# A graph network on one core: queries made with the table's rows and kept beside the residual rows, norms with shared roots

## The chip, the cores and the metric

The kernel runs on 1 core of a Trainium2 chip as one launch. The metric is the device time in microseconds (us). A core has five engines with queues of their own: TensorE (PE; its weight loads are listed as PEld), VectorE (DVE), ScalarE (ACT), GpSimd (POOL, which here issues the gathers and scatters by index) and SyncE (SP, which here issues most transfers). Matmuls write to PSUM, everything else works from SBUF, and transfers (DMA) move data to and from the chip's memory (HBM).

## The reference

There are 6250 nodes with 64 features, 200000 edges sorted by their target, and 64 features per edge.

```python
x = layernorm(x + L0(x, edge_weight, src, dst))      # attention over edges, max and mean of features, a gate
# L1, on that x:
edge_attr = mlp(ln(edge_embed))
for l in range(3):
    h = ln(x)
    q = h[dst] @ Wq[l];  kn, vn = h[src] @ Wkn[l], h[src] @ Wvn[l]
    ke, ve = edge_attr @ Wke[l], edge_attr @ Wve[l]      # all in 8 heads of 8
    alpha = (q * (kn + ke)).sum(-1) / scale
    alpha = softmax of alpha over the edges of one target
    agg = sum over a target's edges of (vn + ve) * alpha
    gate = sigmoid(agg @ Wih[l] + h @ Whh[l])
    x = x + (agg + gate * (h @ Wself[l] - agg)) @ Wout[l]
    x = x + mlp(ln(x))
return layernorm(x + ln(x_after_3_layers) * ng + nb)      # this x: the input of L1
```

(The biases are left out here; the kernel has them.)

## The kernel before

Nodes are sorted by their number of edges and cut into 49 blocks of 128 (the last, LB, has fewer nodes; the spare places of its 128 rows take edges of block 0's fullest nodes). A node of a block sits on a partition, and its edges are slots along the free axis, so a block has a rectangle of 128 x SL[b] edge slots (24 slots that are summed from a table in SBUF, plus 12 to 32 whose rows are gathered or handled with them).

Stage A (0 to about 4780 us) computes L0, the edge features (edge_attr, written to memory in the blocks' slots as `ea_d`), one-hot matrices `oh_d`, and for each block the first layer's inputs by `prepare`. Its order is a written-out schedule over ORDER.

Then come the three layers of L1, in a loop over the blocks in LORDER (L53) as a software pipeline written out by hand: an iteration works on five blocks at once, b (newest) to b4 (oldest), and the order of the calls is the order on every queue.

- `begin` (L1243) loads, for the block of the next iteration, `hv` (the normed features, transposed, with a row of ones) and `xb` (residual rows, from `x1_d` in layer 0 and `x2_d` after it), in layer 2 also `xv` from `x1_d`. The table `ftb` in SBUF holds the blocks' rows of k and v for a layer; `refill` (L1253) fills it from `tab`.
- For block b, TensorE first makes the query `q` (L1489) from `hv` into a PSUM tile `b_qe`, then `sums` makes k and v of the edges in groups of up to 8 slots: edge features by weights (L1310, f32), table rows by one-hot matrices (L1329, bf16, three parts to a number), gathered rows (L1317). ScalarE copies k and v out (L1333, L1336). `scores` (L1340, L1341) multiplies k by q and reduces on VectorE.
- `gather` (L1233) lets GpSimd fetch up to 12 rows of 128 (one `indirect_dma_start` for each) from the table `tab`, into one of 4 buffers; it is called after a part that used such a buffer. One call's gathers are a burst.
- b1: `soft` (L1345 on: maximum, exponent into the same PSUM tile `b_qe`), `values` (L1353 on: weighted sum).
- b2: `turned`, `gate`, `gated` (four VectorE instructions after a tanh, L1397 on), `update` (L1406, L1407).
- b3: `updated` adds the update to the residual rows (L1410) and norms them (`norm`, L531, ten VectorE instructions on 64 columns or on one); `turned2` (L559), `hidden` (L1421, L1423), `close` (L1428 on) adds the MLP's result.
- b4: `prepare` (L573) makes the next layer's inputs: a norm, a transposition (L589) into `fht` with its store, the product with the k and v weights (L601, 128 columns) that ScalarE copies twice (L602, L603), three bf16 parts of it (L608, L611, L614), and the store of the row into `tab`. The norm and the first step are issued from `close`, while the block is still b3. In layer 2 `close` norms twice instead, with the affine of ng, nb and the residual between them (L1437 on), and `put` (L1455) scatters the rows to the output, by index on GpSimd.

The six steps of L1497 to L1501 are spread over the groups of block b, so that TensorE has sums to do between them. Stores of a block are kept in a list `stores` and issued on SP by `flush` at the end of an iteration. Inverse roots are computed on VectorE by two Newton steps (`rsqrt`, L515), whose products are one instruction each for one column (L523) and two for more (L525, L526).

## Time and profile before

| | us |
|---|---|
| median of 3 runs | 10610.52 (10577.22 to 10615.33) |
| profiled execution | 10601.41 |
| its span | 10599.5 |
| layer 0, about | 4830 to 6733 |
| layer 1, about | 6733 to 8632 |
| layer 2, about | 8632 to 10600 |
| PE busy (PEld beside it) | 6784.7 (4613.5) |
| DVE busy | 5774.5 |
| ACT busy | 3190.8 |
| POOL busy | 3983.4 |

The mean granted clock of TensorE was 0.753 of full speed over the whole, and 0.77 to 0.79 in the layers. The profile's lines name a group of equal instructions by source line, engine, operation, output and input; "<-" after a wait names what ended it. "issue" is time in which an engine waited for nothing that the profile shows, "remote" an event that it can't tie to a work of this core. The 40 slices of the span stand as tenths of busy time:

```profile
PE   2544645555555555576677777677777766677776
DVE  5544545544555555553556555455665545666666
POOL 5244333333333333313434444343444434434442
```

Stage A ends in the eighteenth or nineteenth slice; the layers are the rest. TensorE is the busiest engine there.

### The profile page before, as it was taken

The page shows a single profiled execution, that of the slowest core. Times are in us where ns is not written, and L with a number is a line of the kernel's source. Part 1 is how long each engine was busy: PE and PEld are TensorE (multiplying, and loading weights), DVE is VectorE, ACT ScalarE, POOL GpSimd, SP SyncE. Part 2 cuts the span into 40 slices and gives each one's busy share as a digit, 9 for nine tenths or more (in the row PEclk, how much of TensorE's full clock was granted, in tenths as well). Part 3 has the DMA queues.
Part 4 walks back from the last instruction along what each step waited for, and adds up shares of the span by engine and source line. Part 5 has one row for each costly group of instructions (what it writes and reads, how often), then busy time and mean ns, then how long its engine had stood idle before and what let it go on. Part 6 is the DMA issues. An engine that isn't in the chain of part 4 may idle for free.

```text
span 10599.5 us, 163737 instructions
## 1 busy us (share of the span) xinstructions
PE 6784.7 (64%) x62377; PEld 4613.5 (44%) x62377; DVE 5774.5 (54%) x14777; ACT 3190.8 (30%) x6591; POOL 3983.4 (38%) x4201
## 2 busy tenths in 40 slices
PE   2544645555555555576677777677777766677776
PEld 1212222222222222234566666455666655565565
DVE  5544545544555555553556555455665545666666
ACT  1322323322333333342233333223333322222222
POOL 5244333333333333313434444343444434434442
PEclk6676767777777777787787888777778777787877
DMA  4333333333333333334444444444444444444443
GB/s 102 94 89 92 95 89 96 92 90 95 92 91 93 92 91 92 91 87 138 122 128 133 136 136 134 125 123 129 133 134 136 135 130 118 119 126 125 129 127 86
DMA packets 1118549, 1183.96 MB, mean 112 GB/s; under 512 B 669364, under 2 KB 821433, under 8 KB 1110719
## 3 DMA queue, kind: packets, MB, share of 16 engines
q1 hardware_dynamic: 652271, 705.16, 23.3%
q0 software_dynamic: 174624, 393.35, 14.5%
q10 hardware_dynamic: 290864, 74.87, 3.4%
q8 instruction: 502, 8.22, 0.3%
q14 instruction: 288, 2.36, 0.1%
HBM read 936.40 MB, written 236.44 MB: 111 GB/s over the span
## 4 chain that ended last, share of the span: by engine, by line
PE 53%; another core or an unknown queue 19%; issue 17%; ACT 5%; DVE 3%; DMA 1%; POOL 0%; SPq 0%; ACTq 0%; POOLq 0%; DVEq 0%
PE b_pk L1329 18%; PE b_pk L1310 12%; PE f_ph L982 6%; PE b_pk L1317 4%; PE f_tr L945 4%; PE f_pe L964 3%; ACT f_hid L986 2%; ACT s_bc L827 1%; ACT ea L968 1%; PE p_pm L824 1%; ACT f_sq L747 1%; PE p_pm L1421 1%; ACT f_xt L949 1%; PE p_pm L1430 1%
## 5 line engine op out<-in xcount | busy, mean ns | idle before, releaser
L1239 POOL DMA_INDIRECT g<-tab,fidx x2328 | 2245.7, 965 | 3530.2 <-PE b_pk L1317 1720.3
L728 POOL DMA_INDIRECT g<-ft_d,si x1596 | 1522.5, 954 | 2843.0 <-PE e_pt L1045 2370.4
L1329 PE MATMUL b_pk<-ftb,ohl 128*128 128x128 bf16 x21168 | 1889.7, 255 | 881.0 <-issue 830.5
L1329 PEld LDWEIGHTS <-ohl 128*128 128x128 bf16 x21168 | 1592.1, 116 | 1190.5 <-issue 1118.4
L1310 PE MATMUL b_pk<-fwkv,eal 64*128 64x128 f32 x12990 | 1390.8, 316 | 491.0 <-issue 460.2
L1340 DVE TENSOR_TENSOR b_k<-b_k,b_qe 128x768 f32<-128x768 f32 (+6 forms) x711 | 542.0, 762 | 1690.4 <-ACT b_k L1333 1143.9
L964 PE MATMUL f_pe<-f_hid,fw 128*64 128x448 f32 (+4 forms) x2464 | 770.9, 645 | 1080.1 <-ACT ea L968 563.4
L1333 ACT COPY b_k<-b_pk 128x384 f32<-128x384 f32 (+2 forms) x1011 | 475.5, 470 | 3072.4 <-remote 1455.5
L1310 PEld LDWEIGHTS b_pk<-fwkv,eal 64*128 64x128 f32 x12990 | 1064.4, 208 | 719.2 <-issue 634.5
L982 PE MATMUL f_ph<-f_xt,fw 64*128 64x448 f32 (+4 forms) x2464 | 826.1, 678 | 457.8 <-ACT f_xt L949 382.3
L949 ACT ACTIVATE f_xt<-f_tr,feg 128x352 f32<-128x352 f32 (+10 forms) x392 | 253.8, 648 | 2220.2 <-remote 1913.5
L1333 ACT COPY b_v<-b_pk 128x384 f32<-128x384 f32 (+2 forms) x1011 | 872.8, 863 | 0.0
L986 ACT ACTIVATE f_hid<-f_ph,fb 128x448 f32<-128x448 f32 (+4 forms) x1232 | 725.5, 635 | 448.7 <-PE f_ph L982 281.0
L964 PEld LDWEIGHTS f_pe<-f_hid,fw 128*64 128x64 f32 x2464 | 155.1, 149 | 1570.2 <-issue 849.6
L945 PE MATMUL f_tr<-f_mv,f_xs 128*64 128x44 f32 (+10 forms) x12544 | 557.7, 249 | 396.0 <-issue 349.7
L932 DVE TENSOR_TENSOR f_mv<-s_tt,e_fac 128x704 f32<-128x704 f32 (+10 forms) x392 | 349.7, 892 | 778.9 <-remote 663.2
L945 PEld LDWEIGHTS f_tr<-f_mv,f_xs 128*64 128x64 f32 x12544 | 506.3, 160 | 506.1 <-issue 430.4
L982 PEld LDWEIGHTS f_ph<-f_xt,fw 64*128 64x128 f32 x2464 | 261.7, 212 | 822.0 <-ACT f_xt L949 501.2
L1341 DVE TENSOR_REDUCE b_al<-b_k 128x96 f32<-128x768 f32 (+6 forms) x711 | 542.9, 764 | 24.5
L1360 DVE TENSOR_REDUCE b_ag<-b_v 128x64 f32<-128x2816 f32 (+17 forms) x147 | 455.5, 3099 | 5.1
L1359 DVE TENSOR_TENSOR b_v<-b_v,b_qe 128x2816 f32<-128x2816 f32 (+17 forms) x147 | 454.1, 3089 | 0.0
L1317 PE MATMUL b_pk<-g,oh 128*128 128x384 bf16 (+3 forms) x2358 | 446.7, 326 | 0.0
(403 smaller groups left out, 7784.8 us busy)
## 6 DMA issues: line engine op xcount, KB each, us to landing
ohl<-oh_d SPq DMA_DIRECT2D x882, 256.0 KB
eal<-ea_d SPq DMA_DIRECT2D x324, 384.0 KB
oh_d<-s_oh SPq DMA_DIRECT2D x294, 256.0 KB
g<-tab,fidx POOLq DMA_INDIRECT x2328
eal<-ea_d SPq DMA_DIRECT2D x93, 320.0 KB
ea_d<-ea ACTq DMA_DIRECT2D x114, 256.0 KB
eal<-ea_d SPq DMA_DIRECT2D x114, 256.0 KB
ea_d<-ea ACTq DMA_DIRECT2D x130, 224.0 KB
```

What stands on the lines that cost most here:

```text
L728: nc.gpsimd.indirect_dma_start(out=g[:, k - k0, :], out_offset=None, in_=t0_d[:], in_offset=bass.IndirectOffsetOnAxis(ap=got[b]["si"][:, k ...
L945: nc.tensor.matmul(pv[r * D : (r + 1) * D, j], xss[(4 * ORDER.index(b) + 4 * j0 // D) % 4][:, (j0 + j) % (D // 4), :], mv[:, j, :, r::2], ...
L964: nc.tensor.matmul(pe[h * D : (h + 1) * D, :w], w2[:, s, :], hid[s][:, h, :w], start=(s == 0), stop=(s == 1))
L982: nc.tensor.matmul(ph[h][:, :w], w1[r, s * P : (s + 1) * P], xf[r, e0 * D : e1 * D], start=True, stop=True)
L986: nc.scalar.activation(hid[s][:, h, :w], ph[h][:, :w], AF.Relu, bias=b1[:, s : s + 1])
L1239: nc.gpsimd.indirect_dma_start(out=g[:, t - t0, :], out_offset=None, in_=tabs[l % 2][:], in_offset=bass.IndirectOffsetOnAxis(ap=idx[:, f : ...
L1310: nc.tensor.matmul(pk[:, j % 2, j // 2, :], ea[r, e, :], w["wkv"][r], start=(j < 2), stop=False)
L1317: nc.tensor.matmul(pk[:, h, :c, :], ohs[l, b, NW][:, 0, :], rows_[:, slice(t, t + 2 * c - 1, 2), i, :], start=False, stop=(i == 2))
L1329: nc.tensor.matmul(pk[:, h, j, :], o, rows[:, i, :], start=False, stop=(j == c - 1 and q == len(us) - 1 and i == 2))
L1333: nc.scalar.copy(to.rearrange("p (j h) d -> p h j d", h=2), pk[:, :, : n // 2, d0 : d0 + D])
L1340: nc.vector.tensor_tensor(k, k, m["q"].unsqueeze(1).to_broadcast([P, k1 - k0, D]), ALU.mult)
L1341: nc.vector.tensor_reduce(m["al"][:, :, k0:k1].rearrange("p h k -> p k h"), k.rearrange("p k (h d) -> p k h d", h=H), AX.X, ALU.add)
```

## The change

- **The order of blocks** (LORDER): four of the blocks with the fewest edges lead, where two did.
- **The query**: `prepare` makes q, k and v in one product of 192 columns; its q columns are stored beside the residual rows (`x1_d`, `x2_d`, now 128 columns wide, by one DMA more on SP, in `stores`), and `begin` loads both in one transfer. The query's matmul of the layers (L1489) goes; `scores` reads q from SBUF. PSUM's `b_qe` keeps the exponents only. `b_x` and `xv` have a buffer more.
- **Norms**: the norm after the update (b3) and the next layer's norm (b4), in layer 2 also the two closing norms (of b4 and b5), are made together at the iteration's start, after `soft` of b1 and before its `values`, with one inverse root of two or three columns. `close` only adds (and stores); the second closing norm comes one iteration later, and the last block's alone. The affine of layer 2 takes three VectorE instructions, the norm's own last one included, instead of four.
- **gated** takes three VectorE instructions; only the first reads PSUM.
- **Steps**: `turned` of b2 is issued before b4's step, and `gate` and `gated` of b2 before `turned2` of b3.

```diff
-LORDER = (LB, LB - 1) + tuple(b for i in range(24) for b in ((1, 0, *range(2, 24))[i], LB - 2 - i)) [:-1]
+LORDER = (LB, LB - 1, LB - 2, LB - 3) + tuple(b for i in range(23) for b in ((1, 0, *range(2, 23))[i], LB - 4 - i))[:-1]
...
-x1_d = [dram.tile([P, D], F32, name=f"x1_{b}_d") for b in range(NB)]
-x2_d = [dram.tile([P, D], F32, name=f"x2_{b}_d") for b in range(NB)]
+x1_d = [dram.tile([P, 2 * D], F32, name=f"x1_{b}_d") for b in range(NB)]
+x2_d = [dram.tile([P, 2 * D], F32, name=f"x2_{b}_d") for b in range(NB)]
...
+def norms(wk, items):
+    k, mvs = len(items), []
+    for v, _ in items:
+        s6 = wk.tile([P, 6], F32, name="n_s6", bufs=4)
+        mvs.append(s6)
+        nc.vector.bn_stats(s6, v)
+    mv = wk.tile([P, k, 2], F32, name=f"n_mv{k}")
+    for j, s6 in enumerate(mvs):
+        nc.vector.bn_aggr(mv[:, j], s6)
+    vv = wk.tile([P, 2, k], F32, name=f"n_vv{k}")
+    for i, f in enumerate((KC, KC * K1 * K1)):
+        nc.vector.tensor_scalar(vv[:, i], mv[:, :, 1], f, f * EPS, ALU.mult, ALU.add)
+    r = rsqrt(wk, vv, k, f"n{k}")
+    for j, (_, put) in enumerate(items):
+        put(mv[:, j, 0:1], r[:, j : j + 1])
...
-def prepare(wk, mps, w, b, xb, i, hn=None):
+def prepare(wk, mps, w, b, xb, i, xd, hn=None):
...
-    kf = wk.tile([P, W1], F32, name="p_kf")
+    kf = wk.tile([P, 3 * D], F32, name="p_kf")
...
     def rows():
-        pm = mps.tile([P, W1], F32, name="p_pm")
-        nc.tensor.matmul(pm, ht, w["wc"][:, D : 3 * D], start=True, stop=True)
+        pm = mps.tile([P, 3 * D], F32, name="p_pm")
+        nc.tensor.matmul(pm, ht, w["wc"][:, : 3 * D], start=True, stop=True)
-        nc.scalar.copy(part[:, 0], kf)
+        nc.scalar.copy(part[:, 0], kf[:, D:])
+        stores.append(lambda: nc.sync.dma_start(xd[b][:n, D:], kf[:n, :D]))
+        if b == 0:
+            stores.append(lambda: nc.sync.dma_start(xd[LB][LN:P, D:], kf[:SPARE, :D]))
-    nc.vector.tensor_tensor(rest, kf, part[:, 0], ALU.subtract)
+    nc.vector.tensor_tensor(rest, kf[:, D:], part[:, 0], ALU.subtract)
...
-        stores.append(lambda: nc.sync.dma_start(x1_d[b][:], xb))
-        yield from prepare(wk, mps, nxt, b, xb, 0, hn)
+        stores.append(lambda: nc.sync.dma_start(x1_d[b][:, :D], xb))
+        yield from prepare(wk, mps, nxt, b, xb, 0, x1_d, hn)
...
     def begin(l, b):
-        xb = wk.tile([P, D], F32, name="b_x", bufs=6)
-        nc.sync.dma_start(xb, (x1_d if l == 0 else x2_d)[b][:])
+        xq = wk.tile([P, 2 * D], F32, name="b_x", bufs=7)
+        nc.sync.dma_start(xq, (x1_d if l == 0 else x2_d)[b][:])
-            xv = wk.tile([P, D], F32, name="xv", bufs=6)
-            nc.sync.dma_start(xv, x1_d[b][:])
-        ms[b] = dict(hv=hv, xb=xb, xv=xv)
+            xv = wk.tile([P, D], F32, name="xv", bufs=7)
+            nc.sync.dma_start(xv, x1_d[b][:, :D])
+        ms[b] = dict(hv=hv, xb=xq[:, :D], q=xq[:, D:], xv=xv)
...
         def gated(b, m):
-            nc.vector.scalar_tensor_tensor(gt[:, 1], at, 0.5, pg[:, 0], op0=ALU.mult, op1=ALU.add)
-            nc.vector.scalar_tensor_tensor(gt[:, 2], at, -0.5, pg[:, 0], op0=ALU.mult, op1=ALU.add)
-            nc.vector.tensor_mul(gt[:, 2], gt[:, 2], gt[:, 0])
-            nc.vector.tensor_add(gt[:, 1], gt[:, 1], gt[:, 2])
+            nc.vector.scalar_tensor_tensor(gt[:, 1], gt[:, 0], 1.0, pg[:, 0], op0=ALU.add, op1=ALU.mult)
+            nc.vector.scalar_tensor_tensor(gt[:, 2], gt[:, 0], -1.0, at, op0=ALU.add, op1=ALU.mult)
+            nc.vector.scalar_tensor_tensor(gt[:, 1], gt[:, 2], -0.5, gt[:, 1], op0=ALU.mult, op1=ALU.add)
-        def updated(b, m):
-            nc.vector.tensor_add(m["xb"], m["xb"], m["po"][:, :D])
-            m["h2"] = wk.tile([P, D], F32, name="b_h2")
-            norm(wk, m["h2"], m["xb"])
+        def plain(to, v):
+            return v, lambda mean, r: nc.vector.tensor_scalar(to, v, mean, r, ALU.subtract, ALU.mult)
+        def normed(b3, b4, b5):
+            items = []
+            if b3 is not None:
+                m = ms[b3]
+                nc.vector.tensor_add(m["xb"], m["xb"], m["po"][:, :D])
+                m["h2"] = wk.tile([P, D], F32, name="b_h2")
+                items.append(plain(m["h2"], m["xb"]))
+            if b4 is not None:
+                m4 = ms[b4]
+                xb = m4["xb"]
+                if l < 2:
+                    hn = wk.tile([P, D], F32, name="p_hn")
+                    items.append(plain(hn, xb))
+                else:
+                    y = m4["y"] = wk.tile([P, 2, D], F32, name="b_y", bufs=3)
+                    nc.vector.tensor_add(m4["xv"], m4["xv"], gb[:, 1, :])
+                    def close_(mean, r):
+                        nc.vector.scalar_tensor_tensor(y[:, 1], xb, mean, gb[:, 0, :], op0=ALU.subtract, op1=ALU.mult)
+                        nc.vector.scalar_tensor_tensor(y[:, 0], y[:, 1], r, m4["xv"], op0=ALU.mult, op1=ALU.add)
+                    items.append((xb, close_))
+            if b5 is not None:
+                y5 = ms[b5]["y"]
+                items.append(plain(y5[:, 1], y5[:, 0]))
+                last.append((b5, P if b5 < LB else LN, y5))
+            if items:
+                norms(wk, items)
+            if b4 is not None and l < 2:
+                m4["next"] = prepare(wk, mps, nxt, b4, xb, (l + 1) % 2, x2_d, hn)
+                m4["then"] = next(m4["next"])
+            if l == 2 and b4 == LORDER[-1]:
+                norms(wk, [plain(y[:, 1], y[:, 0])])
+                last.append((b4, P if b4 < LB else LN, y))
...
-                nc.sync.dma_start(x2_d[b][:], xb)
-                m["next"] = prepare(wk, mps, nxt, b, xb, (l + 1) % 2)
-                m["then"] = next(m["next"])
-                return
-            y = wk.tile([P, 2, D], F32, name="b_y", bufs=3)
-            norm(wk, y[:, 0], xb)
-            nc.vector.tensor_mul(y[:, 0], y[:, 0], gb[:, 0, :])
-            nc.vector.tensor_add(y[:, 0], y[:, 0], gb[:, 1, :])
-            nc.vector.tensor_add(y[:, 0], y[:, 0], m["xv"])
-            norm(wk, y[:, 1], y[:, 0])
-            n = P if b < LB else LN
-            last.append((b, n, y))
+                nc.sync.dma_start(x2_d[b][:, :D], xb)
...
-            b, b1, b2, b3, b4 = [LORDER[i - k] if 0 <= i - k < NB else None for k in range(5)]
+            b, b1, b2, b3, b4, b5 = [LORDER[i - k] if 0 <= i - k < NB else None for k in range(6)]
...
-            do(b3, updated)
+            normed(b3, b4, b5 if l == 2 else None)
...
-                m["q"], m["ex"] = qe[:, :D], qe[:, D : D + c * H].rearrange("p (h k) -> p h k", h=H)
-                nc.tensor.matmul(m["q"], m["hv"], w["wc"][:, :D], start=True, stop=True)
+                m["ex"] = qe[:, : c * H].rearrange("p (h k) -> p h k", h=H)
...
-            steps = [lambda: (do(b4, then), do(b2, turned)),
-                     lambda: (do(b3, turned2), do(b2, gate, gated)), lambda: do(b4, more, then),
+            steps = [lambda: (do(b2, turned), do(b4, then)),
+                     lambda: (do(b2, gate, gated), do(b3, turned2)), lambda: do(b4, more, then),
```

Only changed lines are shown, with four leading spaces less.

## The prediction

> **What bounds the kernel now.** I read the windows of the three layers first, then TensorE's waits, then the timeline around one burst of gathers, then the groups of the instructions the change touches. Stage A (to about 4780 us) changes only by a wider product and a few stores. Columns: stretch and its length, then busy time (and count) of PE, PEld, DVE, ACT, POOL, then granted clock, DMA share, GB/s.
>
> ```profile
> 4830.00:6733.00 1903.00, 1424.23 (x14105) 1134.40 (x14102) 1079.59 (x2312) 572.69 (x1337) 720.36 (x746) 0.79 0.48 134
> 6733.00:8632.00 1899.00, 1416.78 (x14049) 1133.22 (x14048) 1079.90 (x2310) 564.99 (x1321) 750.27 (x778) 0.78 0.47 131
> 8632.00:10600.00 1968.00, 1388.08 (x13862) 1106.43 (x13860) 1199.96 (x2835) 526.16 (x1125) 791.43 (x821) 0.77 0.43 119
> ```
>
> TensorE is busy 75% of a layer (1424 of 1903), VectorE 57%, DMA under half. What TensorE waits for in 4900 to 10600 (us in total, times, longest):
>
> ```profile
> PE b_pk L1329 <- issue: 851.0, 1149, 2.5
> PE b_pk L1310 <- issue: 459.7, 614, 2.5
> PE p_pm L559 <- DVE b_h L540: 38.9, 9, 10.1
> PE b_qe L1489 <- issue: 23.4, 26, 1.8
> PE p_pm L589 <- DVE p_hn L540: 19.7, 8, 2.8
> PE b_pk L1329 <- DMA ohl<-oh_d: 17.5, 2, 9.8
> ```
>
> VectorE stops TensorE only some 60 us in all, in a few waits; 1,311 us (851 + 460) are "issue", waits for nothing recorded. The timeline says when they come. First GpSimd, then TensorE, in the same ten microseconds:
>
> ```profile
> 6505.38 0.95 POOL L1239 DMA_INDIRECT g<-tab,fidx  x1 [15.65 <-PE b_pk L1317]
> ...
> 6514.18 0.95 POOL L1239 DMA_INDIRECT g<-tab,fidx  x1 [0.30 <-issue]
> 6517.27 0.95 POOL L1239 DMA_INDIRECT g<-tab,fidx  x1 [2.13 <-remote]
> ```
>
> ```profile
> 6510.51 0.43 PE L1489 MATMUL b_qe<-fwc,hv 65*128 65x64 f32 x2
> 6510.88 0.64 PE L1310 MATMUL b_pk<-fwkv,eal 64*128 64x128 f32 x4
> 6512.57 0.47 PE L1310 MATMUL b_pk<-fwkv,eal 64*128 64x128 f32 x2 [1.05 <-issue]
> 6514.03 0.27 PE L1310 MATMUL b_pk<-fwkv,eal 64*128 64x128 f32 x1 [0.99 <-issue]
> 6515.44 0.37 PE L1310 MATMUL b_pk<-fwkv,eal 64*128 64x128 f32 x1 [1.15 <-issue]
> ```
>
> About 5 us after a burst of gathers begins, TensorE starts to issue one or two matmuls per gap of a microsecond, and goes on normally a little after the burst. Over all bursts its gaps above 0.5 us add up to 2.8 us for a burst of 5 gathers, 5.8 for 8, 8.4 for 10, 12.4 for 12, 19.5 for 20: about 1.2 us per gather less 3.7. I call this the stutter. So the layers are TensorE's own instructions plus a stutter that the number and grouping of gathers sets. The change leaves the number alone (776 per layer). What can pay is TensorE instructions outside the stutter, and the ends of layers, where there is no next block to fill TensorE:
>
> ```profile
> 6701.89 0.42 PE L589 MATMUL p_pm<-fident,p_hn 128*64 128x128 f32 x1 [2.12 <-DVE p_hn L540]
> 6704.78 0.39 PE L559 MATMUL p_pm<-fident,b_h 128*64 128x128 f32 x1 [2.14 <-DVE b_h L540]
> ```
>
> **The change part by part.** The groups (count | busy us, mean ns | idle before):
>
> ```profile
> L1489 PE MATMUL b_qe<-fwc,hv 65*128 65x64 f32 x290 | 64.4, 297 | 23.5 <-issue 23.4
> L601 PE MATMUL p_pm<-fwc,fht 65*128 65x128 f32 x196 | 44.4, 310 | 1.1 <-ACT fht L590 1.1
> L1407 PE MATMUL p_pm<-fwout,b_gt 64*128 64x64 f32 x294 | 66.0, 300 | 16.3 <-issue 14.1 <-DVE b_gt L1402 1.3 <-PE p_pm L1406 0.9
> L1340 DVE TENSOR_TENSOR b_k<-b_k,b_qe 128x768 f32<-128x768 f32 (+8 forms) x707 | 539.0, 762 | 1651.2 <-ACT b_k L1333 1104.7 <-issue 298.0 <-ACT b_k L1336 245.2
> L1347 DVE TENSOR_TENSOR b_al<-b_al,fam 128x352 f32<-128x352 f32 (+17 forms) x146 | 76.6, 525 | 1.9
> L523 DVE TENSOR_SCALAR n_t<-n_y,n_vv 128x1 f32<-128x1 f32 x686 | 187.2, 273 | 25.2
> ```
>
> *The query product goes (L1489).* 147 blocks times 2 matmul records, 294. From the start of one to the start of TensorE's next instruction, 238 took at most 0.35 us, 42.4 us together (0.178 each); the other 56 lie in the stutter, 65.2 us together. The first 42.4 are on the path and go. In the stutter the gap belongs to the gathers: another matmul takes the place, and what is saved is that one's ordinary step, 56 x 0.178 = 10 us at most; I take half. Term: -48. Bounds: 0, if it all goes into longer stutter, and -108 (42.4 + 65.2), if the gaps go with their instruction.
>
> *192 columns instead of 128 in prepare's product (L601)*, 147 blocks (49 in stage A, 98 in two layers), 2 records each. In the layers TensorE's step from such a matmul to the next is 202 ns at 128 columns; at 64 (L1407) 201, at 384 (L964, edge features) 207. The width doesn't show in the step. Term 0; bounds 0 and +20, the latter from the mean duration of L964, 645 ns at 448 columns, against 310 here: 335 ns over 320 columns, 67 per 64, x 294. ScalarE copies half as much again; it is busy 30% of a layer, so nothing.
>
> *The q rows' store and the wider load.* One more DMA on SP's queue per block in prepare, 0.32 to 0.36 us to issue; it stands ahead of the table rows' store in the same list, and that waits for VectorE's last part anyway. Behind it are the next block's loads, issued an iteration ahead of their use. Layer 2 has no such stores and stutters no less. In stage A 49 x 0.45 us = +22 is the upper bound; term 0, since TensorE and VectorE there don't wait for SP. The load of residual rows doubles (64 KB for 32, 147 times, 4.8 MB, at a DMA share of 0.48): hidden by being asked for an iteration early; else the residual add would wait for it.
>
> *Scores read q from SBUF (L1340).* Both inputs of the multiply are then in SBUF. The row that is nearest is L1347, two SBUF inputs: of 86 gathers that began within such an instruction 70 took longer, 19.4 us together. Of 102 that began within L1340 (q in PSUM), with 39.5 us of it still to run, none was lengthened. At L1347's rate (19.4 of 31.0 us remaining) that is 25 us more of GpSimd in bursts, and the stutter lasts as long as the burst. Bounds 0 and +40; I take half of the 25, +12, since a stutter already begun may only shift. The multiply itself: L1355 from PSUM takes 519 ns and L1349, the same reduction from SBUF, 522; so no change.
>
> [...]
>
> *Shared norms and gated.* A norm is ten VectorE instructions, 2.45 us from its first to the next instruction (L523 among them at 273 ns). Two with shared roots come to some 3.6 us instead of 4.9, the three of layer 2 to 5 instead of 8.1 (with its affine in fewer instructions); gated loses one of four, 0.3 us. So VectorE does 1.6 us less per block in layers 0 and 1 and 3.5 less in layer 2. In the steady state nothing waits for it: TensorE's waits on L540 above are nine and eight, all in the drains. There VectorE is nearly always busy (6660 to 6705, and 10500 to 10585), and the last blocks' chains, norm to transpose to product, are serial. Worked through, a drain wins about 4 us at each of two layer ends; the last one wins 7, after paying for one norm more that comes alone there. Term: -15; bounds -30 and +10 (the norm now waits for two adds, so the earlier of the pair is late).
>
> *The moved steps.* Norms come after soft(b1) and ahead of values(b1), as the first norm did. The closing norms move to the next iteration's start, ahead of the transposition L589 that was already its first step. Gate before turned2, and turned before then: TensorE swaps neighbours; gated's L1399 waits for the tanh 418 us in all today with nothing behind it that TensorE needs within 1.5 us. Term 0, in those bounds.
>
> *The order of blocks.* Four light blocks lead each layer instead of two. The start burst is 33 gathers instead of 34, the 9.8 us wait for one-hot rows comes from weights' loads that stay, and the last three blocks swap places. Term 0, bounds +-15.
>
> **Sum**, on the profiled execution: 10601.4 - 48 - 15 + 12 = 10550. It was 9 us under the median of the runs shown, 10610.5; to that 10550 is -0.57%.
>
> **The rivals.**
>
> *Nothing reaches the end.* TensorE's 48 us are taken up by stutter: the burst is triggered by TensorE's progress, so with fewer instructions between bursts more of what remains falls into them. For it: five sixths of TensorE's lost time is stutter (1,311 us of 1,541 not busy). Against: the stutter's length goes with the count of gathers, whatever instructions fall in it. Then only drains and lengthened gathers are left, -15 + 12: 10598.
>
> *A larger gain.* All 108 us of the query product go, and the drains give 15: 10478. For it: 26 of the gaps end at L1489 itself (23.4 us of issue). Against: the same gaps end at L1310 and L1329 when these are next.
>
> *Bursts merge (slower).* In 95 of some 106 pairs a block's second burst follows the first by 2.1 us, as at 6517.27: its release at about 6510.2 comes 4.8 us after the first began, while TensorE's signals go unseen from about 4.3 us on. If TensorE is half a microsecond earlier there, the bursts join to one of 16, whose stutter is 1.2 x 16 - 3.7 = 15.5 against 2 x 5.8 = 11.6, and the pause between is lost: some 4.3 us a pair. It costs as much as this change gives from 12 pairs on, and makes the kernel slower by over 0.5% (10663) from 26 pairs; a third of them (35) gives 10700. For it: the margin is small, and the steps between were reordered. Against: the query product stands after that release, not ahead of it.
>
> **How the numbers follow.** About 0.5% is what a measurement of this kernel can tell from no change: 10557 to 10663. Forecast 0.48 (10520 to 10580, of which two thirds are under 10557); nothing reaches the end 0.20; larger gain 0.13; merged bursts 0.19. Faster: 0.31 + 0.13 = 0.44. Same: 0.17 + 0.20 = 0.37. Slower: 0.19. The range goes from the larger gain, 10470, to 10650: that leaves out most of the merged bursts and the edge of the larger gain.
>
> **What would show it.** No L1489; prepare's matmul with 192 columns and a step of about 0.2 us. Layers of 1885, 1882 and 1945 us in the windows. TensorE's issue waits on L1310 and L1329 at 1,290 to 1,340 us; at 1,360 or more the first rival or the merging holds, and pauses of 2.1 us between bursts that are gone tell which. Mean duration of gathers in the layers up by 10 ns (25 us over 2,328) if the multiply holds them up. DVE busy down by some 150 to 200 us with little to show for it. The prediction is wrong if TensorE shows new waits on the norms (L559 or L589 in the middle of layers), or if stage A is longer by more than 10 us.

## The result

| | before | changed |
|---|---|---|
| median of 12 runs each (us) | 10603.47 | 10632.12 |
| lowest to highest | 10577.22 to 10615.33 | 10612.6 to 10642.61 |
| profiled execution's span | 10599.5 | 10629.3 |
| stage A, to the first matmul of layer 0's sums | 4849.0 | 4870.2 |

The ratio is 1.003, with a 95% interval of 1.0023 to 1.0038: slower by 0.3%, where 0.57% less had been forecast. That is within the half per cent that the prediction calls no change, and on the other side of it.

A second pair of profiles, from chip 13 (median of the changed kernel 10626.9, ratio 1.0023, 1.0014 to 1.0033), lets me average. Between the two kernels the span grows by 32.2 us: stage A 19.6 more; from the first to the last matmul of the sums, layer 0 9.9, layer 1 19.7 and layer 2 5.7 more; the two stretches between layers 9.0 less together; the end, from the start of the last sum, 13.7 less (66.0 to 52.3).

The layers' windows of the changed kernel, with the columns of the prediction's first fence:

```profile
4851.00:6756.00 1905.00, 1398.88 (x14005) 1091.61 (x14004) 991.53 (x2073) 583.30 (x1337) 728.99 (x746) 0.78 0.48 135
6756.00:8673.00 1917.00, 1397.00 (x13938) 1095.10 (x13938) 991.18 (x2071) 574.68 (x1321) 761.84 (x778) 0.78 0.47 131
8673.00:10629.00 1956.00, 1361.22 (x13776) 1061.95 (x13775) 1009.21 (x2214) 529.15 (x1125) 804.04 (x822) 0.77 0.43 121
```

TensorE is busy for 72 us less in the three layers (4157 for 4229) and VectorE for 368 us less (2992 for 3359), and the layers are no shorter: 5778 for 5770 us. TensorE's waits of the changed kernel in the layers say where the time went (L1349 is the old L1329, L1330 the old L1310, L606 and L576 the old L589 and L559):

```profile
PE b_pk L1349 <- issue: 1256.8, 1616, 2.6
PE b_pk L1330 <- issue: 213.8, 318, 6.3
PE p_pm L606 <- DVE p_hn L1429: 29.1, 8, 5.6
PE b_pk L1349 <- DMA ftb<-tab: 13.3, 2, 7.0
PE p_pm L576 <- DVE b_h L1429: 6.2, 3, 3.2
```

"issue" on the two sums is 1,471 us where it was 1,311; the waits on norms (L606, L576) lie at the ends of the layers, but for one of 1.0 us. The 160 us are more than the 72 us saved.

The same in steps, each from the start of a matmul to the start of the next, from layer 0's first sum to layer 2's last, averaged over two profiles of each kernel: steps of at most 0.35 us fell from 3533 to 3461 us together, longer ones rose from 2150 to 2248 us. So TensorE's ordinary work gave 72 us, and the longer steps, most of them stutter (1953 of 2152 us in the first profile of before), took 98.

GpSimd's gathers, of the kernel before and then of the changed one (count | busy us, mean ns | idle before):

```profile
L1239 POOL DMA_INDIRECT g<-tab,fidx x2289 | 2208.6, 965 | 3329.4 <-PE b_pk L1317 1720.3 <-issue 620.9 <-PE p_pm L1406 455.8
```

```profile
L1259 POOL DMA_INDIRECT g<-tab,fidx x2295 | 2246.1, 979 | 3396.3 <-PE b_pk L1337 1779.8 <-issue 627.3 <-PE p_pm L1425 451.7
```

They are 14 ns longer each. And pairs of bursts join. Here is one, first the start of the second burst in the kernel before, with a pause of 2.40 us, then the same pair in the changed kernel's timeline, ten gathers from 8024.45 and the second burst after 0.31 us:

```profile
7938.26 0.95 POOL L1239 DMA_INDIRECT g<-tab,fidx  x1 [2.40 <-remote]
```

```profile
8024.45 0.95 POOL L1259 DMA_INDIRECT g<-tab,fidx  x1 [16.42 <-PE b_pk L1337]
...
8036.03 0.95 POOL L1259 DMA_INDIRECT g<-tab,fidx  x1 [0.30 <-issue]
8037.29 1.06 POOL L1259 DMA_INDIRECT g<-tab,fidx  x1 [0.31 <-issue]
```

Of 108 pairs beyond the heavy blocks 0, 1 and 2, one was joined before, 14 and 12 in the two profiles of the changed kernel. To price them I took, for each of 93 pairs that stand alone in both kernels, the window from the first gather to 8 us after the last, less the usual steps of the matmuls that began in it: what TensorE lost there. The second profile of before differs from its first by 1.5 us over all 93 together, so this measure repeats well. The newly joined pairs lost 48 and 39 us more (3.3 each); the 78 to 80 pairs that did not change state lost 53 and 57 more (0.7 each).

### The profile page after: what moved, and what is told of

It reads as the page before. It is cut to its first block, busy times and chain, and to the rows that moved or that the text cites. A ratio compares the mean times of both kernels' runs of the same rounds, so it can differ in the third digit from the quotient of the medians.

```text
span 10629.3 us, 162212 instructions
## 1 busy us (share of the span) xinstructions
PE 6733.2 (63%) x62083; PEld 4496.9 (42%) x62083; DVE 5409.1 (51%) x13678; ACT 3220.5 (30%) x6591; POOL 4015.4 (38%) x4201
## 5 line engine op out<-in xcount | busy, mean ns | idle before, releaser
L1259 POOL DMA_INDIRECT g<-tab,fidx x2328 | 2277.5, 978 | 3525.3 <-PE b_pk L1337 1779.8
L1349 PE MATMUL b_pk<-ftb,ohl 128*128 128x128 bf16 x21168 | 1950.7, 252 | 1275.5 <-issue 1237.6
L1349 PEld LDWEIGHTS <-ohl 128*128 128x128 bf16 x21168 | 1559.2, 114 | 1663.0 <-issue 1610.3
L1360 DVE TENSOR_TENSOR b_k<-b_k,b_x 128x768 f32<-128x768 f32 (+9 forms) x711 | 545.2, 767 | 2185.0 <-ACT b_k L1353 1331.4
L1330 PE MATMUL b_pk<-fwkv,eal 64*128 64x128 f32 x12990 | 1318.8, 318 | 238.2 <-issue 213.8
L1353 ACT COPY b_k<-b_pk 128x384 f32<-128x384 f32 (+2 forms) x1011 | 475.4, 470 | 3192.4 <-remote 1369.8
L1330 PEld LDWEIGHTS b_pk<-fwkv,eal 64*128 64x128 f32 x12990 | 1037.3, 211 | 426.8 <-issue 361.2
L1353 ACT COPY b_v<-b_pk 128x384 f32<-128x384 f32 (+2 forms) x1011 | 875.1, 866 | 0.0
L1361 DVE TENSOR_REDUCE b_al<-b_k 128x96 f32<-128x768 f32 (+9 forms) x711 | 542.9, 764 | 24.5
```

The lines of the kernel that those rows point to most:

```text
L1259: nc.gpsimd.indirect_dma_start(out=g[:, t - t0, :], out_offset=None, in_=tabs[l % 2][:], in_offset=bass.IndirectOffsetOnAxis(ap=idx[:, f : ...
L1330: nc.tensor.matmul(pk[:, j % 2, j // 2, :], ea[r, e, :], w["wkv"][r], start=(j < 2), stop=False)
L1349: nc.tensor.matmul(pk[:, h, j, :], o, rows[:, i, :], start=False, stop=(j == c - 1 and q == len(us) - 1 and i == 2))
L1353: nc.scalar.copy(to.rearrange("p (j h) d -> p h j d", h=2), pk[:, :, : n // 2, d0 : d0 + D])
L1360: nc.vector.tensor_tensor(k, k, m["q"].unsqueeze(1).to_broadcast([P, k1 - k0, D]), ALU.mult)
L1361: nc.vector.tensor_reduce(m["al"][:, :, k0:k1].rearrange("p h k -> p k h"), k.rearrange("p k (h d) -> p k h d", h=H), AX.X, ALU.add)
```

## The experiments

The chips turned out to be of two kinds, which is a result in itself. On chips 8, 10 and 13, as the record numbers them (before at 10536, 10537 and 10602 us; the chip of the first result, at 10603, has no number there), TensorE stutters during bursts; on chips 3 and 4 (6888 and 6891 us) it doesn't (steps over 0.35 us in the layers: 2152 us in the first profile of before, 419 in rows_kept). Each chip was used at one time only, so whether this is the chip or its state at that time isn't shown. Ratios are against the kernel before on the same chip.

**The query's part and the rest, each alone.**

q_alone, the query's edits on the kernel before:

```diff
-            nc.tensor.matmul(pm, ht, w["wc"][:, D : 3 * D], start=True, stop=True)
+            nc.tensor.matmul(pm, ht, w["wc"][:, : 3 * D], start=True, stop=True)
+            stores.append(lambda: nc.sync.dma_start(xd[b][:n, D:], kf[:n, :D]))
...
-            ms[b] = dict(hv=hv, xb=xb, xv=xv)
+            ms[b] = dict(hv=hv, xb=xq[:, :D], q=xq[:, D:], xv=xv)
...
-                    nc.tensor.matmul(m["q"], m["hv"], w["wc"][:, :D], start=True, stop=True)
```

> The kernel before, with the query's part of the change alone: product of 192 columns, q stored beside the residual rows, wider load, no product in the layers, scores read SBUF; norms, gated, steps and block order as before. Theory 1 and theory 2 alike: gathers 978 ns, some 13 joined pairs more than before, TensorE's busy time in the layers down by 50 to 70 us, its gaps up by 85; 10600 to 10650, no drain gain. Rival (the norms, moved steps or the order of blocks join the bursts): no joined pairs more, gaps up by 30 only; about 10580.

no_q, the changed kernel with these edits undone:

> The changed kernel without the query's part: norms with shared roots, gated, steps and order of blocks as changed; q made by its product in the layers, into PSUM. Theory 1 and 2: gathers 965 ns, joined pairs as before (16), only the drains are shorter, by 23 us in all: 10580. Rival (norms, steps or order join the bursts): joined pairs as in the changed kernel, about 10630. Stage A, which both theories leave as it was before: first sum at 4849 and not at 4870 us if the wider rows and their stores cost 21 us there.

q_psum, the changed kernel with q copied to PSUM, from where VectorE's multiply reads it as before the change:

```diff
-                    m["ex"] = qe[:, : c * H].rearrange("p (h k) -> p h k", h=H)
+                    m["ex"] = qe[:, D : D + c * H].rearrange("p (h k) -> p h k", h=H)
+                    nc.scalar.copy(qe[:, :D], m["q"])
+                    m["q"] = qe[:, :D]
```

> The changed kernel, with one thing added: ScalarE copies the loaded q rows (64 columns) to the PSUM tile b_qe at the block's start, and the scores' multiply reads it from there, as before the change. Theory 1 (the multiply with both inputs in SBUF lengthens the gathers, and the longer bursts also meet the second release, so pairs join): gathers of the layers go back from 978 to 965 ns, groups of gathers that follow without a pause go from 29 back to about 16, TensorE's gaps over 0.5 us in the layers from 1170 back to 1085 us; 85 us less than the changed kernel, 10545. Theory 2 (the bursts join because TensorE has no query product any more, wherever q is read): gathers go back, but the joined pairs stay; only some 30 us less, 10600.

old_order, the changed kernel with the old LORDER:

```diff
-LORDER = (LB, LB - 1, LB - 2, LB - 3) + tuple(b for i in range(23) for b in ((1, 0, *range(2, 23))[i], LB - 4 - i))[:-1]
+LORDER = (LB, LB - 1) + tuple(b for i in range(24) for b in ((1, 0, *range(2, 24))[i], LB - 2 - i)) [:-1]
```

> The changed kernel with the order of blocks from before. If the order of blocks makes the pairs join or costs at the layers' start: 10600 or less. If it is nothing, as the prediction had it: 10625 to 10640, with joined pairs in about the same blocks (14, 15, 16, 21, 24).

Measured on chip 10, before at 10537.05 us (all gathers of the layers; "close" are groups that follow the one before without a pause; in the two earlier pairs of profiles the kernel before has 16 of them and the changed one 29 and 27):

| | ratio | interval | gather, ns | close | first sum, us |
|---|---|---|---|---|---|
| q_alone | 1.0011 | 1.0001 to 1.002 | 978 | 23 | 4846 |
| no_q | 1.0002 | 0.9993 to 1.0012 | 970 | 29 | 4843 |
| q_psum | 1.0016 | 1.0004 to 1.0028 | 970 | 26 | 4843 |
| old_order | 1.0042 | 1.0028 to 1.0057 | 976 | 33 | 4836 |

What follows. Neither half pays: the query's part alone is 12 us slower, just clear of noise, though it takes 294 matmuls away and the prediction's terms for it come to -36 (-48 + 12); all the rest together is nothing, though its drains are 23 us shorter (its profile's end from the last sum is 52.1 us, a stretch between layers 37.8). Theory 2 and its rival each had a half of the truth on the joined pairs: the query's part makes 7 close groups more, the norms, steps and order 13, and copying q to PSUM takes 3 of the changed kernel's 29 away. So they came with each of these shifts of the instructions around them; the kernel before stood where few joined.

The gathers are another matter: with q in PSUM they are back at what no_q has.

```profile
L1259 POOL DMA_INDIRECT g<-tab,fidx x2285 | 2217.5, 970 | 3286.7 <-PE b_pk L1337 1734.5 <-issue 620.4 <-PE p_pm L1425 445.5
```

The multiply itself, from SBUF, takes what it took from PSUM (766 ns for 762):

```profile
L1360 DVE TENSOR_TENSOR b_k<-b_k,b_x 128x768 f32<-128x768 f32 (+9 forms) x710 | 544.2, 766 | 2151.8 <-ACT b_k L1353 1331.4 <-issue 568.3 <-ACT b_k L1356 250.3
```

In the changed kernel 89 gathers began inside the scores' multiply and 75 of them were lengthened, 25.7 us together; in the kernel before none of 102. But q_psum as a whole is no faster than 1.0016, so those 26 us did not come through as time either, or ScalarE's copy and the other shifts ate them; this run can't tell which. Old_order suggests that the new order helps by some 0.1 to 0.2%, but the changed kernel itself was measured on other chips, and the intervals overlap: left open.

**Bursts put apart.** before_apart and after_apart, with before_again and after_again as the unchanged kernels for profiles on that chip, 13:

```diff
-            todo[b] = [(b, 0, 12, "o", 0), (b, 12, NW, "o", 0)]
+            todo[b] = [(b, 0, 12, "o", 0)]
...
+                if t0 == 0:
+                    todo[b].append((b, 12, NW, "o", 0))
...
```

(The line left out at the end calls `gather` when table slots follow a gathered part.)

> The kernel before, unchanged, for a profile on the same chip as the next three. All theories: the same time as before within 15 us, 16 groups of gathers that follow without a pause, gathers at 965 ns.

> The changed kernel, unchanged, on the same chip as the other three. All theories: slower than before by 0.2 to 0.4%, about 29 groups without a pause, gathers at 978 ns. If stage A really pays 20 us for wider rows and stores, its first sum comes 15 to 25 us later than that of the kernel before on this chip; if that was one execution's scatter, within 8 us.

> The kernel before, with the two gathered parts of a block put apart: table slots 0 to 12, first gathered part, table slots 12 to 24, second gathered part (before: both gathered parts at the end). The second burst is then released some 15 us after the first one and can't join it. Theory (what a burst costs is set by its own gathers, joined pairs cost 2 to 4 us more): no joined pairs in the middle of layers; time between 40 us less (only the few joined pairs and the overlap of two neighbouring stutters) and 100 us less than before. Rival (the stutter is a fixed cost per gather, however grouped): within 15 us of before.

> The changed kernel with the gathered parts put apart in the same way, so that no pairs can join. Theory (the joined pairs took the gain): faster than before_apart by 25 to 60 us, as TensorE's 50 to 70 us of work and the shorter drains come through, less 30 us of longer gathers. Rival (the change costs in every burst by itself, joined or not): within 10 us of before_apart, or slower.

Measured, before at 10601.68 us: after_again 1.0023 (1.0014 to 1.0033), before_apart 1.0274 (1.0257 to 1.0291), after_apart 1.0147 (1.013 to 1.0164). In before_apart's timeline the second burst now comes 8.30 us after the first, as meant:

```profile
7763.32 0.95 POOL L1241 DMA_INDIRECT g<-tab,fidx  x1 [10.16 <-PE p_pm L1408]
...
7773.40 0.95 POOL L1241 DMA_INDIRECT g<-tab,fidx  x1 [0.30 <-issue]
7782.66 0.95 POOL L1241 DMA_INDIRECT g<-tab,fidx  x1 [8.30 <-PE p_pm L559]
```

No pair joins, and the kernel is 285 us slower: the expectation of 40 to 100 us less was wrong in sign. A pair that is apart loses more than one with the short pause: bursts that stand alone lose 10.3 us with 10 gathers and 8.6 with 8, 18.9 together; a pair of 10 and 8 with a pause of 2 us loses 16.9, and a joined one 20.0 (the latter two over the kernels on stuttering chips). After_apart is 133 us faster than before_apart, so in that surrounding the same change gains 1.2%: what it is worth depends on where the bursts fall.

One number bears on this. From the start of a pair's first burst to TensorE's first step over 0.6 us, in 111 pairs, TensorE gets through 56.6 matmuls in 5.42 us (before), 58.0 in 5.46 (changed), 60.2 in 4.46 (before_apart), 60.7 in 4.57 (after_apart). The count varies by 5 to 9% within a kernel, time by 12 to 19%. In these kernels the free run at the head of a burst is more a number of matmuls than a time. In before_apart it is filled with shorter matmuls, so the stutter starts a microsecond earlier.

**The second burst held back.** The joined pairs were to be taken out of the changed kernel alone: ScalarE reads a column of the buffer that the second burst overwrites, after it has copied out the next block's first group.

```diff
-            last = []
+            last, held = [], []
...
                     sums(m, part, u0, u1)
+                    if j == 0 and held:
+                        nc.scalar.copy(wk.tile([P, 1], F32, name="pace"), held.pop()[:, 0, :1])
+                        gather(l)
...
-                            gather(l)
+                            if j + 1 == len(groups) and part[4]:
+                                held.append(gs[l, b, part[4]])
+                            else:
+                                gather(l)
```

> The changed kernel with the second burst of a pair held back, a third time, for a chip where TensorE stutters in bursts. There, theory of the joined pairs: 0.3 to 0.55% less than the changed kernel's 1.002 to 1.003, so 0.997 to 1.000 of before. Rival (only the count of gathers matters): 1.001 to 1.004 of before. Without the stutter: 0.956 of before, as in its first two runs.

> The changed kernel without the query's part, and with the second burst held back. On a stuttering chip no_q was 1.0002 of before with 20 joined pairs; theory: without them 0.994 to 0.998. Rival: 0.999 to 1.002. On a chip without the stutter: 0.953 to 0.957, as norms_alone.

Measured on chip 8, which stutters, before at 10535.68 us: after_paced_3 1.0084 (1.0067 to 1.01), no_q_paced 1.0128 (1.0111 to 1.0145). The pause is 6.7 us in the median, no pair is joined, and by the measure above the pairs lose what they lost before the change (0.7 us more over all 93, where the changed kernel lost 98 and 93 more). The kernel is slower all the same. A part of that is the hold's own: once in each layer TensorE waits 8.8 to 10.7 us for the added copy, 29 us of 10621 in all (27 in no_q_paced).

```profile
PE b_pk L1330 <- ACT pace L1549: 29.0, 3, 10.7
```

The windows of after_paced_3's layers:

```profile
4845.00:6729.00 1884.00, 1421.31 (x13951) 1112.83 (x13949) 979.83 (x2034) 581.77 (x1356) 723.49 (x743) 0.78 0.48 134
6729.00:8650.00 1921.00, 1442.52 (x13938) 1129.58 (x13937) 987.00 (x2070) 581.30 (x1359) 759.25 (x776) 0.77 0.47 131
8650.00:10618.00 1968.00, 1429.64 (x13829) 1109.89 (x13829) 1010.88 (x2255) 539.42 (x1182) 807.39 (x825) 0.76 0.44 123
```

TensorE is busy for 4293 us with about the matmuls that took 4157 in the changed kernel: the steps up to 0.35 us are 3556 us together, against 3461 there and 3445 to 3469 in q_psum, q_alone and old_order. No_q_paced has 3629 us of them where no_q has 3529. So what the pairs no longer lose comes back as slower matmuls elsewhere and as the hold's own waits, at a slightly lower granted clock in layers 1 and 2 (0.77 and 0.76 for 0.78 and 0.77). The theory that the joined pairs took the gain falls: they do cost 3 us each where they are, but without them, and even with the 29 us taken off, the kernel is 0.5% above before, where the theory had 0 to 0.3% below.

**The chips without the stutter.** Edits of the same kinds on chips 3 and 4, with rows_kept (the kernel before that also makes, stores and loads q, but still makes it by the product in the layers and reads that from PSUM) and norms_alone (no_q with the old order of blocks):

```diff
 # rows_kept: q_alone with this line kept
+                    nc.tensor.matmul(m["q"], m["hv"], w["wc"][:, :D], start=True, stop=True)
```

> The changed kernel, where the second burst of a block's pair is held back until ScalarE has copied out the first group of the next block (ScalarE reads one column of the buffer that the burst overwrites, after those copies: one copy of 128 x 1 more per block). Theory (13 more joined pairs, some 3 us each, are a large part of the loss): no pair joined in the middle of layers, 35 to 60 us less than the changed kernel, so faster than before by 10 to 30 us. Rival (time lost in a stutter goes with the count of gathers and not with their grouping): within 10 us of the changed kernel, 20 to 35 us slower than before.

> The kernel before with the second burst held back in the same way. Theory: it has only 7 joined pairs to lose and 2.1 us of pause already, so within 20 us of before. Rival (a later second burst costs by itself, as it comes later in the block): 20 us or more slower.

> The kernel before with the query's rows made, stored and loaded (192 columns, one store more, wider loads), but the query's product kept in the layers and the scores reading its PSUM: only the added cost. If the rows cost 20 us in stage A: first sum 20 us later than in norms_alone, and the time 20 to 30 us over before. Rival (the later start of the layers in the changed kernel's profiles comes from elsewhere): within 8 us of before, and of norms_alone at the first sum.

> The kernel before with the shared norms, gated in three and the moved steps, but without the query's part and with the old order of blocks. The drains give 23 us. If the order of blocks is worth 20 us (old_order, without it, was the slowest part of the change): 15 to 30 us slower than before, from pairs joined in mid layer (13 or more beyond before's). If the order is worth nothing: within 8 us of before, as no_q.

> The changed kernel with the second burst of a pair held back, again. On a chip where TensorE stutters during bursts (10.6 ms): theory of the joined pairs: 35 to 60 us less than after_3; rival (only the count of gathers matters): within 10 us of after_3. On a chip without the stutter (6.9 ms): within 15 us of after_3, as there joined bursts cost TensorE nothing.

> The changed kernel, unchanged. On a stuttering chip: 0.2 to 0.4% slower than before. On a chip without the stutter: 4 to 5% faster than before, as norms_alone, if VectorE's shorter work is all that counts there; the query's part makes no more than 20 us of difference to norms_alone.

> The kernel before with the query's rows made, stored and loaded but not used. On a stuttering chip: if stage A pays for the rows, first sum 15 to 25 us later than in norms_alone_2 and the time 15 to 30 us over before; if not, within 8 us in both.

> Shared norms, gated in three and moved steps alone, old order of blocks, no query's part. On a stuttering chip: 15 to 30 us slower than before if the order of blocks is worth 20 us in the changed kernel; within 8 us if it is worth nothing. On a chip without the stutter: 4 to 5% faster than before.

| | chip 4, before 6891.35 | chip 3, before 6887.84 |
|---|---|---|
| changed (after_3) | | 0.9578 (0.9562 to 0.9594) |
| changed, held back | 0.9546 (0.9528 to 0.9563) | 0.9563 (0.9547 to 0.9579) |
| norms_alone | 0.9545 (0.9527 to 0.9563) | 0.9563 (0.9547 to 0.9579) |
| rows_kept | 1.0011 (1.0001 to 1.002) | 1.0013 (1.0003 to 1.0022) |
| before, held back | 0.9997 (0.9988 to 1.0007) | |

Here the change is worth 4.2%, and all of it is the norms' part. Layer 2 is where most of it lies. First rows_kept_2, whose computation in the layers is that of the kernel before, then norms_alone_2:

```profile
5511.00:6820.00 1309.00, 1137.37 (x13817) 962.92 (x13816) 1142.39 (x2687) 508.67 (x1112) 790.49 (x821) 0.92 0.63 181
```

```profile
5438.00:6522.00 1084.00, 1063.31 (x13826) 892.62 (x13825) 963.21 (x2099) 521.55 (x1112) 788.66 (x820) 0.99 0.74 217
```

Without the stutter layer 2 of the kernel before is VectorE's: 1142 of 1309 us busy, and TensorE waits for ScalarE's copies into b_v. TensorE's first two waits of rows_kept_2 in all layers, and then the first of norms_alone_2:

```profile
PE b_pk L1313 <- ACT b_v L1336: 242.6, 107, 14.6
PE p_pm L559 <- DVE b_h L540: 38.9, 9, 10.1
```

```profile
PE b_pk L1327 <- ACT b_v L1350: 31.2, 6, 10.5
```

In layer 2 the wait is 165.7 us in 45 times. At each of them ScalarE's queue shows why its copy is late: ahead of it stands the exponent of `soft` (L1354), which waits for VectorE's subtraction of the maximum (L1353). ScalarE's wait there in layer 2, of rows_kept_2 and then of norms_alone_2:

```profile
ACT b_qe L1354 <- DVE b_al L1353: 346.3, 48, 9.0
```

```profile
ACT b_qe L1368 <- DVE b_al L1367: 110.9, 47, 4.9
```

With 179 us less on VectorE TensorE's wait in layer 2 falls to 12 us, and TensorE becomes the bound: 1063 of 1084 us. Its matmuls, about as many, also take 74 us less, at a granted clock of 0.99 for 0.92. The query's part, which takes TensorE work away, still brings nothing on top: after_3 is 13 us slower than norms_alone_2. TensorE waits more there, 49.9 us for the copies into b_v (31.2 in norms_alone_2) and 43.8 us, 49 times, for the next layer's norm (29.1 us, 8 times). Its gathers are longer, 999 ns here against 959:

```profile
L1259 POOL DMA_INDIRECT g<-tab,fidx x2295 | 2293.1, 999 | 1032.0 <-issue 634.5 <-DMA tab<-p_kv 141.0 <-PE b_pk L1337 120.8
```

```profile
L1256 POOL DMA_INDIRECT g<-tab,fidx x2294 | 2200.9, 959 | 1104.1 <-issue 638.3 <-PE b_pk L1334 235.8 <-DMA tab<-p_kv 140.2
```

Rows_kept shows the price of making, storing and loading q: 8 and 9 us by the ratios. Of that little is in stage A: over both chips the first sum comes at 3135.5 us in the mean of five profiles with the rows and at 3132.4 in that of three without. Holding back the second burst changes nothing here for the kernel before (0.9997), and took at most some 10 us off the changed one.

## Why the prediction was wrong

*The query product, -48.* This step failed. "The first 42.4 are on the path and go": they did leave TensorE's ordinary steps (72 us of these went, 60 of them in steps other than the sums), but they did not leave the time. The sentence that failed is the one against the first rival, "the stutter's length goes with the count of gathers, whatever instructions fall in it". The count stayed at 776 a layer and the long steps rose by 98 us. What falls into the stutter changed: the short one-hot matmuls (old L1329) have 406 us more of the "issue" waits, the edge-feature matmuls (old L1310) 246 less. The free run of about 57 matmuls at a burst's head is why I think so: in it two query matmuls of 0.178 us cost two places, and when they go, two shorter ones take these. That this is the mechanism is argued, not shown. That the query's part alone doesn't pay is shown, by q_alone on a stuttering chip (+12 us, where the terms for it come to -36) and by after_3 against norms_alone_2 on one without. What the rows cost by themselves was measured only on chips without the stutter; even both of the prediction's upper bounds for them, +20 and +22, would turn -36 only into +6.

*Gathers held up by the multiply, +12.* Gathers that begin within the multiply are lengthened, as forecast (75 of 89, where it was none of 102), and the rate was right too (25 us forecast, 25.7 measured). Two things were missed: the subtraction of the maximum in `soft`, old L1350, now catches more gathers (10.8 us of lengthening, where it had 5.7), and no run shows the half that the prediction took off. All excess of gathers over 953 ns is 59 us for 27, so GpSimd's bursts hold 32 us more. How much of it is time remains open, since q_psum, without the multiply's part, is no faster.

*The rows, 0.* Mis-sized by little: rows_kept measured +8 and +9 us, of bounds 0 and +20 for the columns and +22 for the stores. That the width doesn't show in TensorE's step did not hold: in the layers the median step from this product is 253 ns at 192 columns, 202 at 128, which is some 10 us over 196 of them. (Of L964's steps, which stood for 384 columns at 207 ns, a quarter are at most 7 ns and the median is 366.) The product's mean duration grew by 58 ns (368 for 310), where 67 had been the upper estimate:

```profile
L618 PE MATMUL p_pm<-fwc,fht 65*128 65x192 f32 x196 | 55.7, 368 | 3.5 <-ACT fht L607 1.8 <-ACT b_h2t L581 1.1 <-DVE b_gt L1419 0.6
```

Stage A itself was 21 and 18 us longer in the changed kernel's two profiles, over the 10 us that the prediction set as a sign of being wrong, and that makes most of the 32 us there. On chip 13 the kernels with bursts apart differ by 20 us too (first sum at 4838 us without the rows, 4859 with them), and on chip 8 the two that hold the burst back (4844 and 4864). On chip 10 kernels with the rows reach it at 4836, 4843 and 4846 us, and no_q, without them, at 4843. But before_again and before_apart, whose code differs in the layers alone, are 21 us apart on one chip (4859 and 4838). No wait was found that names it; whether it is the rows or scatter between profiles stays open.

*The drains, -15.* Right in kind, and 23 us in size: 4.5 us at each layer's end as forecast (4), 13.7 at the very end (7). No_q, which has them, is still at 1.0002, so its layers or its stage A took them back.

*VectorE's lighter steady state, "little to show for it".* Right on the stuttering chips (368 us less busy, no_q at 1.0002). The 150 to 200 us less that were to show it were too few by the prediction's own figures: 1.6 us a block in two layers and 3.5 in the third come to 328. On the other chip it is worth 4.5%. That bound doesn't stand in the profile of before, but its place does: layer 2, where VectorE was busiest.

*The order of blocks and the moved steps, 0.* Not settled for the order. That steps moved past each other cost nothing by waits is right; that they shift the bursts' releases was not in the sum. No_q has 13 close groups more.

*The rival of joined bursts.* It came true, with 11 to 13 pairs more at 3.3 us (4.3 forecast), around the 12 at which I said it would eat the gain. (The pauses before were 2.3 us in the median of 108 pairs, 85 of them from 1.9 to 2.6, and not 2.1 in 95 of 106.) Yet the reading that it decides fell with after_paced_3 and no_q_paced. A price per pair that was about right did not add up to a time, since TensorE ran slower elsewhere when the pairs were taken apart (steps up to 0.35 us at 3556 us in after_paced_3, for 3461). I have no run that shows why, and can't offer a sum that closes for the layers.

## What to carry to other kernels

Where an engine loses time in a state that its own trace doesn't explain, removing instructions from it need not be worth their duration (294 matmuls less left q_alone 12 us slower); try the edit alone before adding up terms. Test an edit on more than one chip: the same edit here is 0.2 to 0.3% slower on one and 4.2% faster on another, and the part that gains there shows as busy time saved on VectorE on both (368 us in the layers on the one, 179 in layer 2 on the other). Count the pauses between bursts before and after, but test their price as well: pairs that joined lost 3 us each where they stood, and putting them apart again did not win the time back.

## What was not expected of the hardware

- Two chips ran the kernel before in 6888 and 6891 us, at a granted clock of 0.91, the others in 10536 to 10603 at 0.75. In the layers TensorE's steps over 0.35 us come to 2152 us in the one kind (before) and 419 in the other (rows_kept), and the gathers are equally long on both (965 and 962 ns). In the stuttering profile 1953 of the 2152 us begin in bursts or within 2 us after them, stretches that make up 3413 of the layers' 5685 us. Stage A differs too, 4849 us for 3138. What makes the stutter is not shown; the transfers are no slower, those of instructions 0.84 us in the mean for 0.83, those of GpSimd's queue 0.141 for 0.141.
- At the head of a pair's first burst TensorE runs free for 56.6 matmuls in 5.42 us in the mean (before), for 60.2 in 4.46 us in before_apart.
- Two bursts of 10 and 8 gathers cost TensorE 16.9 us with a pause of 2 us between them, 20.0 without a pause, and 18.9 when far apart.
